# Four stacked graph layers on one core: in the attention layer, some second source blocks get a product of their own C in place of two products with B and A

## The chip, the cores and the metric

The program runs on one core of a Trainium2 chip. The time is device microseconds (us) of one execution; the kernel before took 4998.77 us (median of 10 executions, 4990.63 to 5002.31). The lower the better. One more execution was recorded with the profiler, and everything said of single instructions comes from it.

The engines of the core work side by side, each through its own list of instructions in order: PE multiplies matrices (a matmul streams its right operand against weights loaded before, and adds into PSUM), DVE does elementwise work on two inputs, ACT does activations and copies, POOL does some elementwise work and gathers, SP issues the transfers from HBM. [...]

## The reference

A graph of 6250 nodes with 206250 directed edges (100000 random pairs in both directions, and a loop at every node) goes through four layers; after each, x = layernorm(x + layer(x)). The layer that matters here is the last one, attention with four heads of 32 columns:

```python
h = (x @ W).reshape(N, H, C)
a_src = jnp.sum(h * att_src, axis=-1)
a_dst = jnp.sum(h * att_dst, axis=-1)
logits = a_src[src] + a_dst[dst]
logits = jnp.where(logits > 0, logits, NEG_SLOPE * logits)      # 0.2
e = jnp.exp(logits - seg_max[dst])
denom = jax.ops.segment_sum(e, dst, num_segments=N)
msgs = h[src] * (e / (denom[dst] + EPS))[:, :, None]
out = jax.ops.segment_sum(msgs, dst, num_segments=N)
```

The exponential of a leaky sum falls into a factor of the source times a factor of the target, with one pair of factors where the sum is positive and another where it is negative. So a head's sums over edges are two products with 0/1-like matrices: the adjacency counts of the edges whose sum is positive (called B here), and of those whose sum is not (C = A - B), where A is the matrix of edge counts between a block of sources and a stretch of targets.

## The kernel before, in words

The adjacency counts A are made early in the kernel, in blocks of 128 sources, and kept in HBM as bf16 (`adj`). The attention layer (`attend`, from L1134) goes through 4 heads x 6 units of targets = 24 **steps**. A unit is 1024 targets, two groups of 512; the sixth unit of each head has 106 targets more (`more`), with small tiles `Am` and `Bm` and a PSUM tile `sm` of their own. Within a step a loop goes over the 49 source blocks of 128 nodes in **pairs** (`for b in range(0, NB, 2)`); this text numbers them by b/2, pairs 0 to 24, the last with one block alone. So there are 600 pairs.

The work of a pair, in the order in which it is written (no planner moves anything here; each engine goes through its list as the loop writes it):

- SP loads A for the pair three places later (L1283, four buffers).
- ACT makes `r` (L1320), one activation of 128x1024 for each block of the pair: 0 or very large, by the sign of the sum.
- DVE makes B = min(A, r) for both blocks in one instruction (L1327), and C = A - B for the first block only (L1329). `r`, `B` and `C` have two buffers each; a third tile of a name waits until the readers of the first are done.
- PE multiplies (L1347), each term once for each of the two groups, so ten matmuls of 512 columns: B of the first block with its table 0; B of the second block with its table 0; for the second block's other sum, B times `minus` (the negated table 1) and A times table 1, which together stand for C times table 1; and C of the first block with its table 1. With `more`, each of the five terms has a small matmul into `sm` as well (L1349).

After each pair, three "lanes" (`sums`, `news`, `ends`) each make one small piece of other work, written behind the pair's own instructions. `sums` closes the step before: at pair 1 ACT copies half of the finished sums out of PSUM (L1229), at pair 2 DVE copies the other half (L1232), then PE folds them with 16 small matmuls for each group (L1239) and DVE scales them (L1243 to L1248); and behind that it makes the next step's `ad` (four PE transposes, L1216, and an ACT copy, L1213 or L1221, for each group). `news` makes the next head's tables, in units 1 to 5 of each head but the last: DVE L1191, L1193 and L1201, ACT L1196, POOL L1198. `ends` finishes the rows in the last head, so that head has more DVE work than the others. The matmuls of a step sum into four PSUM tiles `s`; the pool of them has six.

Before the first step, on the way into the layer, the factors are made: `t` (whose tile is named "neg", L1168 and L1169) goes through two exponentials on ACT (L1170, L1171), and `s` (a tile of its own, L1174) through L1175 and L1176 into a third (L1177).

Of the kernel before, what the change touches and what calls it, by code (L numbers as in the profile page):

```python
# [9 lines left out]
F32 = mybir.dt.float32  # L10
BF16 = mybir.dt.bfloat16
# [7 lines left out]
P = 128  # L19
# [4 lines left out]
F = 512  # L24
D = 128
HEADS = 4
# [42 lines left out]
def kernel(  # L69
# [9 lines left out]
    nc = tc.nc  # L79
# [9 lines left out]
    NB = -(-N // P)  # L89
# [543 lines left out]
    def general():  # L633
        with ExitStack() as st:
# [12 lines left out]
            def edges(name, rows_of):  # L647
                with tc.tile_pool(name=f"{name}s", bufs=1) as ep, \
# [12 lines left out]
                    for b in range(0, N, F):  # L661
# [3 lines left out]
                        for t in range(T):  # L665
                            ohb = ep.tile([P, F], F32, name="ohb", bufs=2)
                            nc.vector.tensor_scalar(ohb[:, :n], wide[:, :n], float(b), node[:, t : t + 1],
                                                    op0=ALU.add, op1=ALU.is_equal)
                            for slot, M, terms in sums:
                                for k, term in enumerate(terms):  # L670
                                    nc.tensor.matmul(pss[slot, k][:M, :n], term(t), ohb[:, :n],
                                                     start=t == 0, stop=t == T - 1)
                        for slot, M, terms in sums:
                            for k in range(len(terms)):
                                a = acc[:M, slot + k, b : b + n]
                                nc.vector.tensor_add(a, a, pss[slot, k][:M, :n])

# [78 lines left out]
    def fast():  # L756
# [377 lines left out]
        def attend(acc, al):  # L1134


            M = 3 * (CH + 1)
            NP = -(-NB // 2)
            hn = acc[:, 0, 0 : NB * D].rearrange("p (b h c) -> p b h c", h=HEADS, c=CH)
            flat = acc[:, 1:3, :].rearrange("p k n -> p (k n)").bitcast(BF16)  # L1140
            US = (2 * NB + NB // 2) * M
            tabs = []
# [7 lines left out]
            with tc.tile_pool(name="f3c", bufs=1) as one, tc.tile_pool(name="f3", bufs=2) as ep, \  # L1150
# [19 lines left out]
                nc.scalar.activation(us[:, :, :, 0], t, AF.Exp)  # L1170
                nc.scalar.activation(us[:, :, :, 1], t, AF.Exp, scale=SLOPE)  # L1171
                nc.vector.tensor_scalar(bias, al[:, 0], BIG, None, op0=ALU.mult)
                s = one.tile([P, NB, HEADS], F32, name="s")
                nc.vector.tensor_add(s, al[:, 1], mids)  # L1174
                nc.vector.tensor_scalar(vs[:, :, :, 0], s, 1.0 - SLOPE, 0.0, op0=ALU.mult, op1=ALU.min)  # L1175
                nc.vector.tensor_scalar(vs[:, :, :, 1], s, SLOPE - 1.0, 0.0, op0=ALU.mult, op1=ALU.min)  # L1176
# [27 lines left out]
                def width(of):  # L1204
                    return sum(rows * nb for n0, rows, nb in of)

                def targets(k, h, n0, of, more):

                    to = one.tile([P, 2 * F + P], F32, name=f"ad{k % 2}")
                    last = None  # L1210
                    for m0, rows, nb in of + more:
                        if last is not None:
                            nc.scalar.copy(*last)  # L1213
                        pt = pps.tile([P, F], F32, name="na")
                        for j in range(nb):
                            nc.tensor.transpose(pt[:, j * rows : (j + 1) * rows],  # L1216
                                                al[:rows, 1, m0 // P + j, h : h + 1].to_broadcast([rows, P]),
                                                ident[:rows, :rows])
                        last = (to[:, m0 - n0 : m0 - n0 + rows * nb], pt[:, : rows * nb])
                        yield  # L1220
                    nc.scalar.copy(*last)  # L1221
                    ready[k] = to
# [30 lines left out]
                class Lane:  # L1253
# [15 lines left out]
                    def rest(self):  # L1269
                        while self.left:  # L1270
                            self.step(self.due)
# [24 lines left out]
                for k, (h, n0, of, more) in enumerate(steps):  # L1296
                    ad, n, m = ready.pop(k), width(of), width(more)
                    tab, minus = tabs[h % 2]
                    s = [[sps.tile([P, F], F32, name="s") for g in of] for _ in range(2)]
                    sm = rps.tile([P, 2, P], F32, name="sm") if more else None  # L1300
                    ns = -(-n // (2 * P))
                    w = n // ns
                    begun = set()
                    if k + 1 < len(steps):
                        sums.add(targets(k + 1, *steps[k + 1]))
                    if n0 == 0:
                        news.rest()
                    if n0 == units[min(1, len(units) - 1)][0] and h + 1 < HEADS:
                        news.add(tables(h + 1, groups))
                    for b in range(0, NB, 2):  # L1310
                        kk = min(2, NB - b)
                        while k == 0 and made < 4 * min(len(groups) + 1, b // 8 * 2 + 4):
                            next(first[made % 2], None)
                            made += 1
                        load(i + 3)
                        At, Am = A.pop(i), more_of.pop(i, None)
                        i += 1
                        r = ep.tile([P, 2, 2 * F + P], BF16, name="r")
                        for l in range(kk):
                            nc.scalar.activation(r[:, l, : n + m], ad[:, : n + m], AF.Relu,  # L1320
                                                 bias=bias[:, b + l, h : h + 1], scale=BIG)

                        def wide(x):
                            return x[:, :kk, :n].rearrange("p l (s q) -> p s l q", q=w)

                        bt = ep.tile([P, 2, 2 * F], BF16, name="B")
                        nc.vector.tensor_tensor(wide(bt), At[:, :ns, :kk, :w], wide(r), ALU.min)  # L1327
                        ct = ep.tile([P, 2 * F], BF16, name="C")
                        nc.vector.tensor_sub(ct[:, :n].rearrange("p (s q) -> p s q", q=w), At[:, :ns, 0, :w],  # L1329
                                             bt[:, 0, :n].rearrange("p (s q) -> p s q", q=w))  # L1330
                        if more:
                            bm = ep.tile([P, 3, P], BF16, name="Bm")
                            nc.vector.tensor_tensor(bm[:, :kk, :m], Am[:, :kk, :m], r[:, :kk, n : n + m], ALU.min)
                            nc.vector.tensor_sub(bm[:, 2, :m], Am[:, 0, :m], bm[:, 0, :m])
                        terms = [(0, tab[:, b, 0], lambda c0, c1: bt[:, 0, c0:c1], lambda: bm[:, 0, :m])]
                        if kk == 2:
                            terms += [
                                (0, tab[:, b + 1, 0], lambda c0, c1: bt[:, 1, c0:c1], lambda: bm[:, 1, :m]),
                                (1, minus[:, b // 2], lambda c0, c1: bt[:, 1, c0:c1], lambda: bm[:, 1, :m]),
                                (1, tab[:, b + 1, 1], lambda c0, c1: At[:, c0 // w : c1 // w, 1, :w], lambda: Am[:, 1, :m])]  # L1340
                        terms.append((1, tab[:, b, 1], lambda c0, c1: ct[:, c0:c1], lambda: bm[:, 2, :m]))
                        for j, (to, row, rhs, rest) in enumerate(terms):
                            row = row.rearrange("p k c -> p (k c)")
                            stop = b + 2 >= NB and all(q[0] != to for q in terms[j + 1 :])
                            for g, (m0, rows, nb) in enumerate(of):
                                c0, c1 = m0 - n0, m0 - n0 + rows * nb
                                nc.tensor.matmul(s[to][g][:M, : c1 - c0], row, rhs(c0, c1), start=to not in begun, stop=stop)  # L1347
                            if more:
                                nc.tensor.matmul(sm[:M, to, :m], row, rest(), start=not begun, stop=stop,  # L1349
                                                 skip_group_check=True)  # L1350
                            begun.add(to)
                        now += 1
                        for lane in (sums, news, ends):
                            lane.step(now)
                    sums.rest()
                    sums.add(close(h, of + more, [[s[to][g][:M, : of[g][1] * of[g][2]] for to in range(2)] for g in range(len(of))]
                                   + [[sm[:M, to, :m] for to in range(2)] for g in more]))
                    sums.due = now + 2
# [58 lines left out]
```

## Time and profile before

| what | value |
|---|---|
| median of 10 executions | 4998.77 us |
| the profiled execution, its own time | 4998.32 us |
| its span, first to last instruction | 4996.5 us |
| first matmul of the attention steps | 3413.71 us into the span |
| steps 1 to 17 (the rest of heads 0 to 2) | 3501.47 to 4545.36, 1043.89 us |
| one of these steps with 1024 targets | 59.4 to 61.0 us, by the starts of the first matmuls |
| one of these steps with 1130 targets (`more`) | 67.3 to 67.6 us |
| head 3, steps 18 to 22 | 59.4, 62.6, 63.5, 64.5 and 62.5 us |

A line of the profile's groups names the source line (L1327), the engine, the operation, the tile that it writes and those that it reads, how many there are, their busy time and the mean of one. In the timeline the columns are the start and the duration in us, then engine, line, operation and tiles, with the idle time before it in brackets and what ended that idle time. In the table of waits the columns are who waited, for what, the total in us, how often, and the longest. In the chain of waits each row is a start, a duration and what ran there, with x the number of instructions.

### The profile page before, as it was taken

What the parts mean: (1) busy time and instruction counts of PE and PEld (TensorE: products, weight loads), DVE (VectorE), ACT (ScalarE), POOL (GpSimd) and SP (SyncE); (2) the same over time, 40 slices, a digit from 0 to 9 for tenths busy, and PEclk for the clock granted to TensorE, in tenths of its full rate; (3) what the DMA queues carried; (4) which work ended last, traced back from release to release, by engine and by line L of the source; (5) the groups of instructions that cost most, each with busy time, mean ns of one, the idle gap of its engine ahead of it and who ended that gap; (6) DMA issues with size and microseconds to landing.
All of it is one profiled execution on the core that took longest, in us unless ns stands there. A gap on an engine that the chain in (4) does not pass through costs nothing. (4 is left out here: it accounts for less than half of the span.)

```text
span 4996.5 us, 90752 instructions
## 1 busy us (share of the span) xinstructions
PE 4716.9 (94%) x33855; PEld 3924.5 (79%) x33855; DVE 3020.2 (60%) x5084; ACT 2602.9 (52%) x3617; POOL 2010.6 (40%) x1966
## 2 busy tenths in 40 slices
PE   4999998999999999999999999996999999999994
PEld 3899997999999999999999988994556556556553
DVE  6888875344444444444444432225888888888998
ACT  4444443333333333333333321005998999999884
POOL 3333432777777777777777740001110110110000
PEclk9999999999999999999999999997999999999997
DMA  6333333555555555555555545553777777777773
GB/s 105 128 131 134 142 134 122 149 154 155 154 153 155 155 154 153 155 156 154 152 156 154 154 153 180 184 190 107 217 218 227 215 217 227 212 220 223 210 213 108
DMA packets 599589, 834.35 MB, mean 167 GB/s; under 512 B 119837, under 2 KB 484313, under 8 KB 594917
## 3 DMA queue, kind: packets, MB, share of 16 engines
q1 hardware_dynamic: 513077, 603.59, 39.1%
q0 software_dynamic: 85072, 224.21, 15.2%
q8 instruction: 272, 4.46, 0.4%
q14 instruction: 176, 1.44, 0.1%
q10 hardware_dynamic: 992, 0.66, 0.0%
HBM read 738.23 MB, written 89.88 MB: 166 GB/s over the span
## 5 line engine op out<-in xcount | busy, mean ns | idle before, releaser
L127 POOL DMA_INDIRECT g<-t,src_i x1617 | 1590.3, 983 | 506.4 <-issue 397.8
L1320 ACT ACTIVATE r<-ad,bias 128x1024 bf16<-128x1024 f32 (+1 forms) x1176 | 1276.6, 1155 | 90.1 <-DVE B L1327 55.8
L1347 PEld LDWEIGHTS <-acc 128*99 128x99 bf16 x5856 | 697.4, 126 | 604.6 <-issue 156.5
L1095 DVE TENSOR_TENSOR g<-g,pre 128x512 f32<-128x512 f32 x882 | 553.5, 642 | 1018.6 <-PE pre L1093 651.7
L1347 PE MATMUL s<-B,acc 128*99 128x512 bf16 x3504 | 884.6, 382 | 88.7 <-DVE B L1327 83.2
L1107 PE MATMUL seg<-oh,g 128*128 128x64 f32 (+1 forms) x6468 | 967.0, 272 | 0.1
L1107 PEld LDWEIGHTS seg<-oh,g 128*128 128x128 f32 (+1 forms) x6468 | 890.6, 193 | 24.3 <-issue 1.2
L1096 ACT ACTIVATE g<-g 128x512 f32<-128x512 f32 x882 | 508.4, 592 | 588.6 <-DVE g L1095 569.6
L1093 PE MATMUL pre<-W1s,eaT 128*128 128x256 f32 (+1 forms) x3234 | 777.6, 382 | 20.2 <-DVE g L1095 20.0
L1327 DVE TENSOR_TENSOR B<-A,r 128x2048 bf16<-128x2048 bf16 x600 | 723.2, 1205 | 117.9 <-ACT r L1320 91.4
L1093 PEld LDWEIGHTS pre<-W1s,eaT 128*128 128x128 f32 (+1 forms) x3234 | 582.2, 191 | 86.3 <-issue 22.5
L1107 PE MATMUL seg<-oh,ea 128*128 128x64 f32 (+1 forms) x3234 | 628.0, 276 | 0.0
L1084 ACT COPY eaT<-tp 128x512 f32<-128x512 f32 (+1 forms) x441 | 242.0, 549 | 705.1 <-PE tp L1082 695.5
L907 ACT CAST A<-pa 128x784 bf16<-128x784 f32 x400 | 324.5, 811 | 350.7 <-PE pa L904 350.5
L1198 POOL TENSOR_TENSOR xs<-xs,acc 128x264 f32<-128x264 f32 (+1 forms) x104 | 105.1, 1018 | 990.8 <-ACT acc L1196 969.4
L1107 PEld LDWEIGHTS seg<-oh,ea 128*128 128x128 f32 (+1 forms) x3234 | 493.7, 193 | 0.0
L798 PE MATMUL sum<-A,xs 128*128 128x256 bf16 (+1 forms) x3675 | 470.7, 274 | 0.4 <-ACT A L907 0.4
L1329 DVE TENSOR_TENSOR C<-A,B 128x1024 bf16<-128x1024 bf16 x600 | 430.9, 718 | 63.6 <-PE s L1347 0.8
L798 PE MATMUL sum<-A,acc 128*128 128x256 bf16 (+1 forms) x3675 | 409.3, 271 | 3.3 <-DMA A<-adj 3.3
L798 PEld LDWEIGHTS <-acc 128*128 128x128 bf16 x3675 | 355.1, 98 | 44.8 <-issue 4.8
L798 PEld LDWEIGHTS <-xs 128*128 128x128 bf16 x3675 | 358.9, 102 | 36.7 <-issue 0.6
L904 PE MATMUL pa<-oh,oh 128*128 128x98 bf16 x3200 | 356.0, 269 | 26.9 <-ACT A L907 22.4
(229 smaller groups left out, 4416.9 us busy)
## 6 DMA issues: line engine op xcount, KB each, us to landing
A<-adj SPq DMA_DIRECT2D x2304, 128.0 KB
ea<-in_edge_attr_dram SPq DMA_DIRECT2D x292, 256.0 KB
A<-adj SPq DMA_DIRECT2D x100, 704.0 KB
ea<-in_edge_attr_dram SPq DMA_DIRECT2D x146, 192.0 KB
g<-t,src_i POOLq DMA_INDIRECT x1617
Am<-adj SPq DMA_DIRECT2D x96, 128.0 KB
A<-adj SPq DMA_DIRECT2D x25, 320.0 KB
t<-y SPq DMA_DIRECT2D x24, 256.0 KB
```

Of the source, the lines that this page charges most:

```text
L127: nc.gpsimd.indirect_dma_start(out=to, out_offset=None, in_=table, in_offset=bass.IndirectOffsetOnAxis(ap=index[:K, t : t + 1], axis=0))
L798: nc.tensor.matmul(ps[:, :n], parts[part][:, b, :], a(b)[:, :n], start=k == 0, stop=k == 3 * NB - 1)
L904: nc.tensor.matmul(ps[:, o, q * LO : (q + 1) * LO], ohs[g][0][:, 2 * j + o, :, q], ohs[g][1][:, 2 * j + o, :, q], start=True, stop=True)
L907: nc.scalar.copy(A[sb][:, :, q0 : q0 + 2 * QI].rearrange("p k (o q) -> p k o q", q=QI), ps[:, :, : QI * LO].rearrange("p o (q k) -> p k o ...
L1093: nc.tensor.matmul(pre[:K, t, :], eaT[i][:, b + t, :K], W1s[:, 1, :], start=True, stop=True)
L1095: nc.vector.tensor_add(gb, gb, pre[:K, :n, :])
L1096: nc.scalar.activation(gb, gb, AF.Relu)
L1107: nc.tensor.matmul(ps[:, m, :], rows, oh[c][:K, a + t, :], start=a + t == 0 and m == 0, stop=a + t == T - 1, skip_group_check=True)
L1320: nc.scalar.activation(r[:, l, : n + m], ad[:, : n + m], AF.Relu, bias=bias[:, b + l, h : h + 1], scale=BIG)
L1327: nc.vector.tensor_tensor(wide(bt), At[:, :ns, :kk, :w], wide(r), ALU.min)
L1329: nc.vector.tensor_sub(ct[:, :n].rearrange("p (s q) -> p s q", q=w), At[:, :ns, 0, :w], bt[:, 0, :n].rearrange("p (s q) -> p s q", q=w))
L1347: nc.tensor.matmul(s[to][g][:M, : c1 - c0], row, rhs(c0, c1), start=to not in begun, stop=stop)
```

## The change

In pairs 2, 7, 12, 17 and 22 (b = 4, 14, 24, 34, 44) of every step of heads 0, 1 and 2, DVE makes C for both blocks of the pair, with a second instruction of the same shape. The second block's other sum is then one term, C times table 1, in place of the two terms with `minus` and A; the pair has four terms in place of five, and the C of both blocks come last. The tile pool is unchanged: "C" has two buffers, and such a pair takes both. With `more`, the small subtraction L1334 covers two rows in place of one (in `Bm`, four rows in place of three), and the small matmul of one term goes too. All other pairs, and head 3, are as before. Apart from that, `s` of the way in takes the tile "neg" of `t` in place of one of its own.

```diff
-                s = one.tile([P, NB, HEADS], F32, name="s")
+                s = one.tile([P, NB, HEADS], F32, name="neg")
...
-                        ct = ep.tile([P, 2 * F], BF16, name="C")
-                        nc.vector.tensor_sub(ct[:, :n].rearrange("p (s q) -> p s q", q=w), At[:, :ns, 0, :w],
-                                             bt[:, 0, :n].rearrange("p (s q) -> p s q", q=w))
+                        cc = kk if b % 10 == 4 and h + 1 < HEADS else 1
+                        ct = []
+                        for l in range(cc):
+                            ct.append(ep.tile([P, 2 * F], BF16, name="C"))
+                            nc.vector.tensor_sub(ct[l][:, :n].rearrange("p (s q) -> p s q", q=w), At[:, :ns, l, :w],
+                                                 bt[:, l, :n].rearrange("p (s q) -> p s q", q=w))
                         if more:
-                            bm = ep.tile([P, 3, P], BF16, name="Bm")
+                            bm = ep.tile([P, 4, P], BF16, name="Bm")
                             nc.vector.tensor_tensor(bm[:, :kk, :m], Am[:, :kk, :m], r[:, :kk, n : n + m], ALU.min)
-                            nc.vector.tensor_sub(bm[:, 2, :m], Am[:, 0, :m], bm[:, 0, :m])
+                            nc.vector.tensor_sub(bm[:, 2 : 2 + cc, :m], Am[:, :cc, :m], bm[:, :cc, :m])
                         terms = [(0, tab[:, b, 0], lambda c0, c1: bt[:, 0, c0:c1], lambda: bm[:, 0, :m])]
                         if kk == 2:
+                            terms.append((0, tab[:, b + 1, 0], lambda c0, c1: bt[:, 1, c0:c1], lambda: bm[:, 1, :m]))
+                        if kk > cc:
                             terms += [
-                                (0, tab[:, b + 1, 0], lambda c0, c1: bt[:, 1, c0:c1], lambda: bm[:, 1, :m]),
                                 (1, minus[:, b // 2], lambda c0, c1: bt[:, 1, c0:c1], lambda: bm[:, 1, :m]),
                                 (1, tab[:, b + 1, 1], lambda c0, c1: At[:, c0 // w : c1 // w, 1, :w], lambda: Am[:, 1, :m])]
-                        terms.append((1, tab[:, b, 1], lambda c0, c1: ct[:, c0:c1], lambda: bm[:, 2, :m]))
+                        for l in range(cc):
+                            terms.append((1, tab[:, b + l, 1], lambda c0, c1, l=l: ct[l][:, c0:c1], lambda l=l: bm[:, 2 + l, :m]))
```

## The prediction

> **What bounds the kernel now.** I read the page first, for the engines' shares; then the busy time in steps 1 to 17 alone, since all of the change but one line lies in heads 0 to 2; then who waits for whom there; then the chain of waits and the timeline through one whole step (step 9, 3989.97 to 4049.69).
>
> ```profile
> PE 4716.9 (94%) x33855; PEld 3924.5 (79%) x33855; DVE 3020.2 (60%) x5084; ACT 2602.9 (52%) x3617; POOL 2010.6 (40%) x1966
> ```
> ```profile
> 3501.47:4545.36 1043.89, 1010.18 (x5207) 614.43 (x5205) 919.50 (x1294) 961.73 (x1023) 89.21 (x78) 1.00 0.73 220
> ```
>
> The page says PE, with DVE at 60%. The second line (length, then busy PE, weight loads, DVE, ACT and POOL, the granted clock, DMA) says otherwise for the stretch that is changed: PE 97%, ACT 92%, DVE 88%. Three engines are nearly full, so what counts is who is late at which place. The waits of the stretch:
>
> ```profile
> PE s L1347 <- DVE B L1327: 25.2, 40, 1.2
> ACT r L1320 <- DVE B L1327: 28.3, 46, 1.6
> ACT ad L1213 <- PE na L1216: 29.8, 17, 2.1
> DVE B L1327 <- ACT r L1320: 52.7, 66, 2.2
> ```
>
> Of the 33.7 us in which PE is idle there, 25.2 end with DVE's B. ACT's `ad` waits once in each of the 17 steps for PE's transposes. So the limit changes hands within a step, and the chain through step 9 shows where:
>
> ```profile
> 3995.47 1.27 DVE sT L1232 x2
> 3996.74 1.14 DVE B L1327
> 3997.88 0.04 issue
> 3997.93 4.48 PE s L1347 x20
> ...
> 4010.15 6.49 PE s L1347 x30
> 4016.64 0.45 PE na L1216 x4
> 4017.09 0.02 issue
> 4017.12 0.59 ACT ad L1213
> 4017.70 2.08 ACT r L1320 x2
> ```
>
> DVE carries it into pair 3, PE from pair 3 to the transposes behind pair 9, ACT from `ad` to pair 22, and then DVE again over the seam into the next step. In every step of 1 to 17 the rows are the same within some tenths, so one step is a fair model of all.
>
> **The prices.** One matmul: the row "4010.15 6.49 PE s L1347 x30" gives 0.216 us. A changed pair drops two of ten: 0.43 us of PE. A C takes 0.69 us, but the instruction behind it starts 0.61 after it did (4009.71 to 4010.32). While POOL's `xs` runs, a C takes 0.97; over the stretch's 400 the mean is 0.723 beside a median of 0.692. So one more C costs DVE's queue 0.61 + 0.03 = 0.64 (bounds 0.61 and 0.89). It waits for no result of the C in front. With `more`, L1334 over two rows is nearest to L1333's 0.265 in place of 0.217: +0.05. Over 18 steps x 5 pairs that is 39 us off PE and 58 us onto DVE. What it does to the end is worked out by pair.
>
> **Pair 2 (DVE binds).** The rows of DVE and PE:
>
> ```profile
> 3994.57 0.97 DVE L1329 TENSOR_TENSOR C<-A,B 128x1024 bf16<-128x1024 bf16 x1
> 3995.47 1.27 DVE L1232 COPY sT<-s 99x512 f32<-99x512 f32 x2
> 3996.66 1.21 DVE L1327 TENSOR_TENSOR B<-A,r 128x2048 bf16<-128x2048 bf16 x1
> 3997.93 0.59 PE L1347 MATMUL s<-B,acc 128*99 128x512 bf16 x2 [1.09 <-DVE B L1327]
> ```
>
> From C of pair 2 over the two copies to B of pair 3 DVE isn't idle (0.00 to 0.04 us in steps 1 to 17), and PE stands idle 0.46 to 1.16 us until that B is done, starting 0.05 after it. The second C goes in front of the copies, so all of it arrives at PE; the 0.43 that PE saves in pair 2 only adds to its idle time. 17 x 0.64 + 3 x 0.05 = +11.0 us. Step 0 has 2.86 us of DVE idle there: nothing. From pair 3 to 11 PE has no idle time, so nothing takes this back.
>
> **Pair 7 (PE binds).** Here 0.43 could be gained. But three C's now share two buffers: C of pair 8 must wait until PE has read the first C of pair 7.
>
> ```profile
> 4009.71 0.69 DVE L1329 TENSOR_TENSOR C<-A,B 128x1024 bf16<-128x1024 bf16 x1
> 4009.99 1.48 PE L1347 MATMUL s<-B,acc 128*99 128x512 bf16 x6
> 4011.60 1.23 DVE L1327 TENSOR_TENSOR B<-A,r 128x2048 bf16<-128x2048 bf16 x1
> ```
>
> The rows are C of pair 8, PE's pair 7, B of pair 9. PE frees that buffer after six of eight matmuls, at 4009.99 + 5 x 0.216 + 0.38 = 4011.45, so with 0.05 to notice it C of pair 8 starts at 4011.50, 1.79 later than now. Queued behind it are the scaling (L1243 to L1248) and B of pair 9, with 0.10 idle to absorb it: B ends 1.69 later, at 4014.52. PE took that B at 4014.32 and would now be free at 4013.89, so it starts at 4014.57: 0.25 late instead of 0.43 early. The same arithmetic gives +0.79, +0.30, +0.25, +0.34 in units 1 to 4, +0.16 in unit 5, +0.03 in unit 0, and -0.43 in step 0, where C of pair 8 comes 5.4 us after that read. Sum 3 x 1.68 + 3 x 0.16 + 2 x 0.03 - 0.43 = +5.1 us. Bounds: -7.7 (18 x 0.43, if the buffer comes free in time) and +9 (0.5 a step). The wait is also in front of `r` of pair 11, but `ad` behind pair 11 waits for PE anyway.
>
> **Pairs 12, 17 and 22 (ACT binds, DVE just follows).** PE's saving is worth nothing: `r` ends 0.03 us before B starts. DVE's idle time from here, without the 0.10 that every C waits for its B, is 1.06, 0.98, 0.92, 0.42 us (units 1 to 4) between pairs 12 and 17: the C of pair 12 is absorbed but for 0.22 in unit 4. Between pairs 17 and 22 it is 0.16, 0.53, 0.58, 0.58, so 0.48, 0.11, 0.06, 0.28 are left when pair 22 adds its 0.64, and the idle time before B of pair 23 (0.37, 0.06, 0, 0) takes little. At the seam there is none:
>
> ```profile
> 4044.81 1.22 DVE L1327 TENSOR_TENSOR B<-A,r 128x2048 bf16<-128x2048 bf16 x1
> 4046.07 4.26 ACT L1320 ACTIVATE r<-ad,bias 128x1024 bf16<-128x1024 f32 x4 [0.33 <-DVE B L1327]
> 4047.03 0.68 DVE L1327 TENSOR_TENSOR B<-A,r 128x1024 bf16<-128x1024 bf16 x1
> 4048.42 1.22 DVE L1327 TENSOR_TENSOR B<-A,r 128x2048 bf16<-128x2048 bf16 x1
> ```
>
> ACT's `r` of the next step's pair 0 waits for B of pair 23 to free its buffer (0.03 us behind it), and behind that `r` stand the one of pair 1, the copies `sT`, the `r` of pair 2 and so pair 2's B. The lag arrives whole at the idle PE of pair 3: 0.75, 0.69, 0.70, 0.92 in units 1 to 4, 3 x 3.06 = 9.2 us; 0.65 and 0.83 in steps 6 and 12; 0.82, 0.60, 0.82 in steps 5, 11, 17, where DVE also carries Bm; 0.15 in step 0, with 0.49 idle. Sum +13.1 us; bounds 0 and 54 x 0.64 = 35.
>
> **The way in.** `s` in the tile of `t` waits for the second exponential (3399.78 + 0.36) in place of starting at 3399.55, and behind it on DVE stand L1175, L1176 and the tables, on ACT the third exponential and `ad`: +0.7 us (bounds 0 and 0.8). SP and POOL get nothing new: A's buffers come free when DVE has read A, no later than now.
>
> **Sum.** 11.0 + 5.1 + 13.1 + 0.7 = +29.9 us on the profiled execution's 4998.3 (span 4996.5 and 1.8 around it, 0.5 below the median): 5028 us.
>
> [...]
>
> **Rivals.**
> - PE sets the pace and DVE's 12% of idle time holds the C's: 4998.3 - 39 = 4959 us. It needs 0.64 us of DVE slack at both places at which I find none; for it stands the 97%, against it the four rows of pair 2. Its milder form, gains in pair 7 and where PE has no wait in pairs 17 and 22 and nothing lost at the seam, ends near 4998.3 + 11 - 18 x 3 x 0.43 = 4986. Together 0.15.
> - The lags are absorbed at the seam and C's two buffers don't hold: pair 2's +11.0, the way in's 0.7 and pair 7's -7.7 give +4, 5002 us, no change to be told. It decides if B of pair 23 isn't what ACT waits for; in 15 of the 18 steps it is, and in the other three (`more`) it is Bm behind that B. 0.11.
> - DVE becomes the bound all through: all 90 C's at 0.64 = 58, 5057 us. Head 3, where DVE is 93% busy, takes 62.5 to 64.5 us a step and shows that such a state exists; against it stand 0.42 to 1.06 us of idle DVE after pair 12. 0.06.
> - That the change doesn't do what it says: the lists are written by the loops, so L1347 must lose 180 matmuls and C gain 90. Not counted.
>
> **How the numbers follow.** My forecast has 0.68, with a range of its own from 5010 (the seam takes half, pair 7 gives 0) to 5044 (C at 0.89). What a measurement can tell from no change is about 0.2%, 10 us. The forecast and the DVE bound are slower, 0.74; the absorbed case is the same, 0.11; the PE cases are faster, 0.15. Leaving out the faster cases and a part of the slowest, the range is 4995 to 5045.
>
> **What the changed profile would show.** PE's idle time before pair 3 up by about 1.8 us (0.43 saved, 0.64 and some 0.75 later); DVE idle with "PE s" as the releaser before C of pair 8, some 1.2 us each; PE waiting for B of pair 9, which it doesn't now; `r` of pair 0 still behind B of pair 23; a step with 1024 targets at 61.5 to 62.5 us instead of 59.4 to 61.0; head 3 unchanged. The prediction is wrong if B of pair 3 comes less than 0.5 us later against the step's last PE wait, or if steps get shorter.

## The result and the profile after

The changed kernel takes 5033.4 us (median of 8 executions, 5024.73 to 5042.28) against 4997.45 us for the kernel before (28 executions): 36 us more, a ratio of 1.0074 with a 95% interval of 1.0065 to 1.0082. It is slower, as forecast, by 36 us where 30 were forecast. The profiled execution took 5028.66 us, its span is 5026.9; of the difference, the attention steps (first to last matmul) make 1555.45 - 1518.95 = +36.5 us, and the layers before them, which the change doesn't touch, happened to be 6.8 us shorter in this execution (up to `bias`, 3392.61 against 3399.38).

Steps 1 to 17 run from 3497.84 to 4574.11 us here. First the busy time of that stretch (length, then PE, weight loads, DVE, ACT, POOL, the granted clock, DMA), then who waited for whom in it (total us, times, longest).

```profile
3497.84:4574.11 1076.27, 987.54 (x5020) 592.25 (x5020) 966.38 (x1379) 965.57 (x1024) 80.37 (x78) 1.00 0.71 213
```
```profile
PE s L1353 <- DVE B L1328: 69.6, 96, 1.9
ACT r L1321 <- DVE B L1328: 63.8, 75, 2.1
DVE B L1328 <- ACT r L1321: 26.8, 43, 1.2
ACT r L1321 <- DVE Bm L1337: 26.3, 24, 2.2
DVE C L1333 <- PE s L1353: 25.3, 33, 1.2
```

PE's busy time fell by 22.6 us (1010.18 to 987.54) and DVE's rose by 46.9 (919.50 to 966.38); the stretch is 32.4 us longer. (The 85 changed pairs of the stretch drop 85 x 0.43 = 37 us of matmuls; the busy time falls by less because the last matmul before an idle time counts for its whole 0.38 us, and there are more idle times now, 196 in place of 95.) PE's waits for DVE's B went from 25.2 to 69.6 us and ACT's from 28.3 to 63.8, while DVE waits half as long for ACT as before (52.7 to 26.8): DVE has become the one that is late. The 25.3 us in which C waits for PE are new. The places of step 9 again, pair 2 first (start, duration; DVE's rows, then PE's first matmul of pair 3):

```profile
4006.29 1.57 DVE L1333 TENSOR_TENSOR C<-A,B 128x1024 bf16<-128x1024 bf16 x2
4007.78 1.28 DVE L1233 COPY sT<-s 99x512 f32<-99x512 f32 x2
4008.98 1.21 DVE L1328 TENSOR_TENSOR B<-A,r 128x2048 bf16<-128x2048 bf16 x1
4010.24 0.38 PE L1353 MATMUL s<-B,acc 128*99 128x512 bf16 x1 [1.74 <-DVE B L1328]
```

Two C's stand in front of the copies, B of pair 3 comes 0.6 later after B of pair 2 (4.02 us in place of 3.42, start to start), and PE idles 1.74 us in place of 1.09. Pairs 7 to 9:

```profile
4023.82 0.69 DVE L1333 TENSOR_TENSOR C<-A,B 128x1024 bf16<-128x1024 bf16 x1 [1.19 <-PE s L1353]
4025.98 1.21 DVE L1328 TENSOR_TENSOR B<-A,r 128x2048 bf16<-128x2048 bf16 x1
4027.24 0.38 PE L1353 MATMUL s<-B,acc 128*99 128x512 bf16 x1 [0.87 <-DVE B L1328]
```

C of pair 8 waits 1.19 us for PE to read the first C of pair 7, and PE then idles 0.87 us for B of pair 9, where it didn't wait before. Pair 17 to 18 shows one thing that I hadn't counted, B of pair 18 at 1.69 us beside POOL's `xs`:

```profile
4045.61 1.29 DVE L1333 TENSOR_TENSOR C<-A,B 128x1024 bf16<-128x1024 bf16 x2
4046.67 0.76 POOL L1199 TENSOR_TENSOR xs<-xs,acc 128x264 f32<-128x264 f32 x1 [2.85 <-ACT acc L1197]
4046.82 1.69 DVE L1328 TENSOR_TENSOR B<-A,r 128x2048 bf16<-128x2048 bf16 x1
4048.57 1.46 PE L1353 MATMUL s<-B,acc 128*99 128x512 bf16 x6 [0.94 <-DVE B L1328]
```

And the seam, where `r` of the next pair 0 waits for B of pair 23, 0.71 us now, 0.33 before:

```profile
4058.54 1.22 DVE L1328 TENSOR_TENSOR B<-A,r 128x2048 bf16<-128x2048 bf16 x1
4059.79 4.26 ACT L1321 ACTIVATE r<-ad,bias 128x1024 bf16<-128x1024 f32 x4 [0.71 <-DVE B L1328]
```

### The profile page after: what moved, and what is told of

Read it like the earlier page. It is cut to its first block, busy times and chain, and to the rows that moved or that the text cites. A ratio compares the mean times of both kernels' runs of the same rounds, so it can differ in the third digit from the quotient of the medians.

```text
span 5026.9 us, 90243 instructions
## 1 busy us (share of the span) xinstructions
PE 4688.7 (93%) x33660; PEld 3896.8 (78%) x33660; DVE 3068.9 (61%) x5174; ACT 2605.3 (52%) x3617; POOL 2002.6 (40%) x1966
## 5 line engine op out<-in xcount | busy, mean ns | idle before, releaser
L1353 PEld LDWEIGHTS <-acc 128*99 128x99 bf16 x5676 | 676.4, 126 | 665.3 <-issue 239.6
L1353 PE MATMUL s<-B,acc 128*99 128x512 bf16 x3324 | 845.8, 382 | 139.2 <-DVE B L1328 132.7
L1333 DVE TENSOR_TENSOR C<-A,B 128x1024 bf16<-128x1024 bf16 x690 | 484.8, 710 | 94.4 <-PE s L1353 32.6
L1353 PE MATMUL s<-C,acc 128*99 128x512 bf16 x1380 | 402.2, 381 | 0.6 <-DVE C L1333 0.2
```

What stands on the lines that cost most here:

```text
L1333: nc.vector.tensor_sub(ct[l][:, :n].rearrange("p (s q) -> p s q", q=w), At[:, :ns, l, :w], bt[:, l, :n].rearrange("p (s q) -> p s q", q=w))
```

## How the runs are read

Every pair starts with a matmul of its own, so the start of each pair can be compared between two profiles, and a difference that grows between two pairs has reached PE there. The table adds up, over steps 1 to 17, what each stretch of pairs gained or lost against the kernel before; step 0 and head 3 stand by themselves. All in us, worked out from the starts of the matmuls in one profiled execution of each kernel.

| run | attention | step 0 | pairs 0-3 | 3-7 | 7-10 | 10-17 | 17-22 | 22 to end | head 3 |
|---|---|---|---|---|---|---|---|---|---|
| the change | +36.5 | +2.5 | +11.1 | -0.7 | +8.3 | +1.3 | +8.5 | +3.9 | +1.6 |
| PE's saving alone | -7.9 | -1.8 | +0.4 | +0.1 | -7.5 | -0.6 | -0.3 | +1.3 | +0.6 |
| DVE's C's alone | +26.1 | -0.6 | +11.0 | -0.5 | 0.0 | +1.2 | +8.8 | +4.2 | +2.1 |
| the change, own buffer | +23.0 | -0.7 | +11.3 | +4.3 | -6.4 | +0.7 | +8.8 | +2.9 | +2.1 |
| pair 2 alone | +11.0 | -0.1 | +10.8 | -0.5 | 0.0 | +0.4 | -0.1 | +0.3 | +0.2 |
| pair 7 alone | -2.1 | -0.3 | +0.7 | -0.1 | -5.7 | +1.0 | +2.0 | -1.0 | +1.3 |
| pair 17 alone | +5.9 | -0.5 | -0.5 | -0.1 | 0.0 | -0.2 | +9.4 | -4.2 | +1.9 |
| pair 22 alone | +8.1 | -1.0 | -0.7 | +0.1 | 0.0 | -0.2 | 0.0 | +8.4 | +1.4 |
| no C in pair 2 | -17.5 | -0.7 | -10.2 | -2.4 | 0.0 | +0.2 | +0.9 | -0.4 | -4.9 |
| no C in pair 2, pair 7 changed | -20.3 | -0.5 | -10.7 | -2.0 | -4.0 | +0.3 | 0.0 | +0.7 | -4.0 |

A column can differ by 1 to 2 us without any doing of the edit: head 3, which the first eight rows leave as it was, differs by +0.2 to +2.1. In the changed kernel (+1.6) one stretch at half clock lies there (granted 0.50 from 4919.95 to 4923.36 us), 1.22 us after PE had waited 1.50 us for B. PE's saving alone, DVE's C's alone, the change with its own buffer and pair 7 alone were run on another chip, on which the kernel before takes 5445.16 us: the granted TensorE clock is lower there ahead of the attention steps (0.94 for the whole execution against 0.98 on the first, with 1.00 in steps 1 to 17 on both). The attention steps run at the same speed on both (in head 3, 90 to 93% of the pairs agree within 0.01 us), so the table holds across them. The other runs were made on chips with 4995.55 and 4993.34 us for the kernel before. Ratios are always against the kernel before on the same chip; the change itself was not run on the slower chip, so its buffers are compared by the attention steps. The runs without a C in pair 2 keep `s` as the kernel before has it, but for the one that also changes pair 7; all others have it in the tile "neg", as the changed kernel does.

## PE's saving by itself, and DVE's price by itself

In all 90 pairs the product with `minus` is left out and no second C is made (the diff is against the changed kernel, as are the others unless it is said):

```diff
-                        cc = kk if b % 10 == 4 and h + 1 < HEADS else 1
+                        cc = kk if False else 1
...
-                                (1, minus[:, b // 2], lambda c0, c1: bt[:, 1, c0:c1], lambda: bm[:, 1, :m]),
+                                *([] if b % 10 == 4 and h + 1 < HEADS else [
+                                    (1, minus[:, b // 2], lambda c0, c1: bt[:, 1, c0:c1], lambda: bm[:, 1, :m])]),
```

> The 90 pairs of the change lose one of their five terms on PE (the product of minus and B, two matmuls of 512 columns, 0.43 us), and DVE makes no second C. The sum of the second block's other half is left out of the output in these pairs. This is PE's saving by itself. My theory: PE sets the pace only from pair 3 to the transposes behind pair 9, so only the saving in pair 7 arrives: 18 x -0.43 = -7.7, with the way in +0.6, about -7 us against the kernel before (4983 to 4993). The rival (PE at 97% sets the pace everywhere): 90 x -0.43 = -39, about 4959 us.

Ratio 0.9989 (0.9964 to 1.0015); attention -7.9 us. Its busy line for steps 1 to 17:

```profile
3948.31:4985.54 1037.23, 981.62 (x5020) 592.35 (x5020) 919.13 (x1294) 962.27 (x1024) 88.28 (x78) 1.00 0.75 221
```

PE is busy 28.6 us less in the stretch than before (1010.18) and the stretch is 6.7 us shorter (1043.89). Step by step the gain is 0.43 to 0.48 us at pair 7 in every one of the 17, and nothing that lasts at pairs 2, 12, 17 and 22. That is what the theory says, and PE's pace as the limit of all pairs (-39) is out.

Then the other half: the second C is made, into a place of its own, and nothing reads it; PE does its ten matmuls.

```diff
+                spare = [W1s.rearrange("p k h -> p (k h)").bitcast(BF16)]
+                taken = 0
...
-                            ct.append(ep.tile([P, 2 * F], BF16, name="C"))
+                            if l:
+                                ct.append(spare[taken % len(spare)])
+                                taken += 1
+                            else:
+                                ct.append(ep.tile([P, 2 * F], BF16, name="C"))
...
-                        if kk > cc:
+                        if kk == 2:
...
-                        for l in range(cc):
+                        for l in range(1):
```

> The second C of the 90 pairs is made, into a place of its own (the space of the W1 table, which only the fallback branch would read again), and nothing reads it; PE does its ten matmuls as before. This is DVE's price by itself, without the C buffers. My theory: pair 2 costs 17 x 0.6 and the lag over the seam some 13 us, pair 7 costs nothing since PE is late there by more than 1 us: +24 us, about 5021 us (5013 to 5029). The rival that the C buffers are the cause of the loss: 4998 us. The rival that DVE is the bound all through: 90 x 0.61 = +55, 5052 us.

Ratio 1.0041 (1.0017 to 1.0065), +22 us by the interval's middle; attention +26.1 us.

```profile
3933.50:5002.02 1068.52, 1013.77 (x5206) 614.35 (x5206) 967.62 (x1379) 965.62 (x1024) 82.16 (x78) 1.00 0.73 215
```

DVE's 48 us more work (967.62 against 919.50) make the stretch 24.6 us longer, with PE's work as before. The table says where: +11.0 into pair 3, nothing at pair 7, +13 between pair 17 and the seam. So most of the loss is DVE's queue at two places, and half of DVE's added time is hidden at the others.

## The two buffers of C

The change with the second C in a place of its own (the `spare`, `taken` and `ct.append` lines of the diff above, all else as in the change):

> The changed kernel with one edit: the second C of a pair goes to a place of its own (the space of the W1 table), so the C of the next pair needn't wait until PE has read the first one. My theory: the +8 us measured between pairs 7 and 10 and the +2.2 in step 0 turn into 18 x -0.43; pair 2 and the seam stay as they are (+10.6 and +12.4): about +16 us against before, 5013 us (5007 to 5019). The rival that the buffers don't matter: 5033 us, as the changed kernel.

Ratio 1.0041 (1.0020 to 1.0062); attention +23.0 us instead of +36.5. Between pairs 7 and 10 the +8.3 turned into -6.4, and step 0 went from +2.5 to -0.7. The 14.7 us between pairs 7 and 10 were the buffers' doing, and of step 0's 3.2 at least a part. About +16 was expected (8 to 20 by the range of times), so this missed, because something new came in at pair 3 of steps 1, 7 and 13: 1.4 us each, the table's +4.3. In step 7, with PE's rows first and then PE busy, the granted clock, DMA share and GB/s in windows there:

```profile
4317.36 0.59 PE L1359 MATMUL s<-W1s,acc 128*99 128x512 bf16 x2
4319.69 2.63 PE L1359 MATMUL s<-B,acc 128*99 128x512 bf16 x6 [1.74 <-DVE B L1330]
4323.53 1.46 PE L1359 MATMUL s<-B,acc 128*99 128x512 bf16 x6
```
```profile
4318.00:4320.00 2.00, 0.31 (x2) 0.95 0.89 257
4320.00:4321.00 1.00, 1.00 (x4) 0.50 0.60 193
4321.00:4322.00 1.00, 1.00 (x4) 0.50 0.05 15
4322.00:4323.00 1.00, 1.00 (x4) 0.50 0.00 0
4323.00:4324.00 1.00, 1.00 (x6) 0.89 0.09 16
```

After PE's 1.74 us of idle time the clock is granted by half for some 3.4 us (0.20, 3.00 and 0.22 by the windows), and six matmuls take 2.63 us instead of 1.46. The buffers are shown as the cause of the loss at pair 7; without these 4.3 us this run would stand at +18.7. (The tile W1s in the first row is the second C of pair 2.)

## One pair at a time

Only pair 7 (`b == 14`), its second C in a place of its own:

> As the run before, but only pair 7 is changed in each step of heads 0 to 2; pairs 2, 12, 17 and 22 are as in the kernel before. My theory: only the pair in which PE is the limit is left, 18 x -0.43 = -7.7 and the way in +0.6: -7 us, about 4990 us (4986 to 4994). The rival that a second C on DVE costs its 0.6 us wherever it stands: 18 x (0.6 - 0.43) = +3, 5001 us.

Ratio 0.9997 (0.9979 to 1.0015); attention -2.1 us. The 0.43 arrives at pair 7 in every step (0.48 with `more`), so the price of 0.6 wherever a C stands is out. But less than half is left at the end: in three steps with `more` 0.37 is lost again at pair 9; in single steps DVE waited for a late A (1.28 us before pair 19 of step 3), or B met POOL's `xs` (1.69 to 1.72 us at pairs 17 and 19 of steps 2 and 14); and head 3, which the edit leaves as it was, took 1.3 more. The gain is real where it is made and too small to survive; by time it can't be told from none.

Only pair 2, and only pair 17, and only pair 22 (`b == 4`, `b == 34`, `b == 44`), in the same way, each with one profiled execution:

> Only pair 2 is changed as in the diff, in heads 0 to 2, its second C in a place of its own. Measured by the attention steps in the profile, first to last matmul, against 1518.95 us before. My theory: DVE isn't idle between C of pair 2 and B of pair 3, so each of 17 steps loses 0.6 us there, as the changed kernel showed: +10 us (9 to 12). If PE were the limit: 18 x -0.43 = -8.

> Only pair 17 is changed in each step of heads 0 to 2, its second C in a place of its own. Measured by the attention steps in the profile, first to last matmul, against 1518.95 us in the kernel before. In the changed kernel PE's matmuls of pair 18 come about 0.6 us late in most steps and stay late to pair 22. My theory: DVE and ACT catch up before the seam (0.16 to 0.58 us of idle DVE time by pair 22 and a little behind it), so by pair 3 of the next step most of it is gone: 0 to +4 us. The rival that PE carries the delay on: 18 x 0.5 = +9 us.

> Only pair 22 is changed, its second C in a place of its own; same measure. My theory: there is no time left to catch up before the seam, where r of the next pair 0 waits for B of pair 23: 0.64 less the idle DVE time in front of that B (0.37, 0.06, 0, 0 in units 1 to 4), so 3 x 2.1 + 2 x 0.45 + 3 x 0.6 = +9 us (6 to 11). The rival that the seam has slack and pair 22 matters only together with pair 17: 0 to +3 us.

Pair 2 alone costs 11.0 us, 0.6 in nearly every step between pairs 2 and 3 (9.6 of the table's 10.8; 1.0 of the rest came before pair 2 of step 1 alone). Pair 22 alone costs 8.1, all of it behind pair 22. Pair 17 alone costs 9.4 us at PE up to pair 22, of which 4.2 are given back at the seam: 5.2. The sum of 5.9 also holds 1.3 for one late transfer at pair 2 of step 11 (DVE waits 1.98 us for A) and 1.9 in head 3, which it leaves as it was. So the delay at pair 17 doesn't vanish as I had it, nor does it all stay. The single pairs add up: 11.0 + 5.9 + 8.1 = 25.0 beside the 26.1 of DVE's C's alone, in which pair 7 costs nothing. Pair 12 wasn't run by itself; the column of pairs 10 to 17 leaves +1.3 at most for it.

## The opposite of the change where DVE is late

If DVE is late before pair 3 and PE idles there, the opposite should win. On the kernel before, with `s` and `Bm` as they were, pair 2 of all steps makes no C at all, and the first block too gets two products (the diff is against the kernel before):

```diff
+            minus4 = [flat[:, 2 * US + k * M : 2 * US + (k + 1) * M].rearrange("p (k c) -> p k c", c=CH + 1) for k in range(2)]
...
+                        if b0 == 4:
+                            nc.vector.tensor_scalar(minus4[h % 2], tab[:, 4, 1], -1.0, None, op0=ALU.mult)
...
+                        cc = kk if False else 1
+                        ct = []
+                        for l in range(0 if b == 4 else cc):
...
+                            if b != 4:
+                                nc.vector.tensor_sub(bm[:, 2 : 2 + cc, :m], Am[:, :cc, :m], bm[:, :cc, :m])
...
-                        terms.append((1, tab[:, b, 1], lambda c0, c1: ct[:, c0:c1], lambda: bm[:, 2, :m]))
+                        if b == 4:
+                            terms += [
+                                (1, minus4[h % 2], lambda c0, c1: bt[:, 0, c0:c1], lambda: bm[:, 0, :m]),
+                                (1, tab[:, b, 1], lambda c0, c1: At[:, c0 // w : c1 // w, 0, :w], lambda: Am[:, 0, :m])]
+                        for l in range(0 if b == 4 else cc):
+                            terms.append((1, tab[:, b + l, 1], lambda c0, c1, l=l: ct[l][:, c0:c1], lambda l=l: bm[:, 2 + l, :m]))
```

> The opposite of the change at the place where DVE is the limit, on the kernel before: in pair 2 of every step, all heads, DVE makes no C at all; the first block too gets two products, B with a negated table (one more small DVE instruction a head) and A with table 1, so PE has twelve matmuls there in place of ten. My theory: B of pair 3 comes 0.61 earlier and PE, which stands idle 0.46 to 1.16 us in front of it, has 0.43 more to do: a gain of the smaller of 0.61 and that idle time less 0.43, 3 x (0.5 + 0.5 + 0.61 + 0.38) + 2 x 0.55 = 7 us in heads 0 to 2 and about 2 in head 3, so attention at 1510 (1507 to 1514) and a ratio of about 0.998. The rival that PE at 97% is the limit: 23 x 0.43 = +10 us.

4973.33 us against 4995.55: ratio 0.9958 (0.9944 to 0.9971), 22 us faster than before and faster than both kernels. Attention -17.5 us, twice what was expected. Step 9, DVE and then PE:

```profile
3984.42 1.28 DVE L1236 COPY sT<-s 99x512 f32<-99x512 f32 x2
3985.92 1.23 DVE L1331 TENSOR_TENSOR B<-A,r 128x2048 bf16<-128x2048 bf16 x1 [0.22 <-DVE sT L1236]
3986.71 0.59 PE L1361 MATMUL s<-A,acc 128*99 128x512 bf16 x2
3987.20 1.02 PE L1361 MATMUL s<-B,acc 128*99 128x512 bf16 x4
```

PE goes from pair 2 (twelve matmuls) into pair 3 at 3987.20 without a gap. I had set the gain too low at one point: the idle time in brackets counts from the end of the last matmul, which is 0.38 after its start, while the next may start 0.216 after it; so PE had 0.16 us more room than the brackets said, and the steps with 1024 targets gained 0.54 to 0.89 at this place. The `more` steps gained 1.2 to 1.35 where I had nothing. In the kernel before, PE waits three times there, before pair 3 for B and in pairs 2 and 3 for `Bm` as well, and in this run none of the three is left (step 5 of the kernel before):

```profile
3748.29 0.21 PE L1349 MATMUL sm<-Bm,acc 128*99 128x106 bf16 x1 [0.30 <-DVE Bm L1333]
3750.87 0.59 PE L1347 MATMUL s<-B,acc 128*99 128x512 bf16 x2 [0.46 <-DVE B L1327]
3751.85 0.21 PE L1349 MATMUL sm<-Bm,acc 128*99 128x106 bf16 x1 [0.39 <-DVE Bm L1333]
```

Head 3 gained 4.9 instead of 2.

The same with pair 7 changed as in the change, its second C in a place of its own; and the same without that, but with no C in pairs 7, 12, 17 and 22 of head 3 either, where DVE has more work:

> The run before together with pair 7 changed as in the diff, its second C in a place of its own: C goes from DVE to PE where DVE is the limit and from PE to DVE where PE is. My theory: 9 us from pair 2 and up to 7.7 from pair 7 (5.7 of it arrived between pairs 7 and 10 in the run with pair 7 alone, and 2 at the end of attention): attention at 1506 us (1502 to 1512), ratio about 0.9975. The rival that PE is the limit: +10 - 7.7 = 1521 us.

> The run without C in pair 2 (ratio 0.9958, attention 1501.5 us), and in head 3 no C in pairs 7, 12, 17 and 22 either: in the head where DVE is 91 to 95% busy the opposite of the change in all its five pairs. My theory: 6 steps x 4 pairs, each worth up to 0.61 of DVE and at least the 0.2 by which it exceeds PE's 0.43, so -5 to -14 us beside that run: attention at 1492 (1487 to 1497), ratio about 0.994. The rival that head 3 is held up by its layernorm's chains and not by DVE's queue: no gain beside that run, or a loss of up to 24 x 0.43 = 10 us.

The first takes 4970.92 us, ratio 0.9956 (0.9943 to 0.9970); attention -20.3. The second takes 4976.49 us against 4993.34, ratio 0.9957 (0.9944 to 0.9971); attention -20.8, of which head 3 makes 8.2 instead of 4.9. Both miss what was expected of them. The first was expected at 1506 us of attention and took 1498.66, but 17.5 of its 20.3 are the run without C in pair 2, and pair 7 adds only 2.8 of up to 7.7: it keeps 4.0 up to pair 10, and head 3, which it doesn't touch, came out 0.9 worse. The second was to gain 5 to 14 us beside the run without C in pair 2 and gained 3.3: in head 3 the 0.43 that PE has to do more shows up in full at pair 7 of every step, and four of the six steps get it back by pair 10. Neither can be told from the run without C in pair 2 alone by its time.

## Why the prediction was right

The forecast of 5028 us met 5033.4, and the loss came at the places named. Not every term held: one is mis-sized, one has the wrong sign, and one came out right in its sum with parts that were not.

- **Pair 2, +11.0.** Measured +11.1 into pair 3, 0.6 in nearly every step, and +11.0 with this pair alone. The step held as written, and the opposite edit gained where this one lost.
- **Pair 7, +5.1, of it +5.6 in steps 1 to 17.** The mechanism, a C that waits for its buffer, is in the profile with 1.19 us and B of pair 9 late behind it; a buffer of its own takes it away. By units: +0.79, +0.30, +0.25, +0.34 were worked out for units 1 to 4, +0.80, +0.28, +0.60, +0.27 came. Two units were mis-sized. In unit 3 (+0.25 against +0.60) L1249, queued behind that C, takes 0.62 us beside POOL's `xs` in each of the three steps, where it took 0.29. In unit 5 (+0.16 against +0.87) PE waits in pair 9 for B and then 0.38 more for `Bm`, which stands behind it in DVE's queue; 0.54 of the 0.87 come there. Sum +8.3.
- **Step 0, -0.3 (-0.43 at pair 7, +0.15 at the seam).** This term was wrong: +2.5. I looked at the wait of pair 8's C only. The second C of pair 7 itself waits, for PE to read the C of pair 6, and in step 0 PE is far behind:

```profile
3433.05 0.69 DVE L1333 TENSOR_TENSOR C<-A,B 128x1024 bf16<-128x1024 bf16 x1 [0.94 <-PE s L1353]
```

  The second C's of pairs 2, 17 and 22 wait 1.90, 1.22 and 1.30 us in that step in the same way. Behind that of pair 7 on DVE stand the tables' products, on which the ACT casts of the first tables wait. With its own buffer step 0 lost nothing. How much of the 2.5 is each wait's isn't shown: step 0 also had the granted clock at half for 31.0 us, against 29.5 before (0.83 on the mean of the step in both). In steps 1 to 17 too the second C of pair 7 waits for the C of pair 6, 0.06 to 0.81 us, which the prediction left out.
- **Pairs 17 and 22 and the seam, +13.1, of it +12.9 in steps 1 to 17.** Measured +12.4 between pair 17 and the end of the step. The sum is right, by luck in part, for its split isn't: I let the delay of pair 17 run out before pair 22 but for 0.06 to 0.48 us, and at PE it stands at 0.5 us or so at once and comes back by less than half at the seam. Two rows were missing. PE has no idle time between pairs 18 and 22 (step 9), so what it loses there it keeps until somebody else is later. And `xs` on POOL met B in place of C: B at 1.69 to 1.73 us instead of 1.22 came 15 times in steps 1 to 17, 5 times before, ten times 0.48 us. I had priced a collision at 0.03 us, by C's mean, which fell meanwhile from 0.729 to 0.716 in the stretch.
- **PE's idle time before pair 3.** It was to rise by some 1.8 us, because the lag would arrive whole there. It rose from 0.87 to 1.63 on the mean of steps 1 to 17, and exactly as far with pair 2 alone; with pair 22 alone it stayed at 0.85. The lag of pairs 17 and 22 reaches PE before the seam, as the table's last columns of a step show, so this part of the path was wrong. And of the 0.43 that PE saves in pair 2, some 0.27 on the mean goes into waiting inside the pair, in step 9 for the second C.
- **The way in, +0.7.** From `bias` to the first `r` it takes 11.36 us instead of 10.74: +0.6.
- **PE's busy time, and B beside `xs`.** The busy time of the matmuls would have given -39 us; PE's saving alone brought 7.9, and the waits said the same. The 1.69 us of B in place of 1.22, beside an `xs` that started 0.15 before it and took 0.76, are 0.47 more for an overlap of 0.61. The term from it, ten such B's more at 0.48, is some 5 us of DVE's time, for which the forecast had its 0.03 a piece, 2.7 for 90 C's. What holds B up beside `xs` isn't shown.

That is 37 us in the attention steps and on the way in (35 from the bullets, 2 from the other columns); 36 by the medians. The rivals are out by their own runs: PE's pace by PE's saving alone, the absorbed lags by pair 22 alone (+8.1) and by the buffers' 1.19 us, DVE as the bound all through by DVE's C's alone (+26 of 55).

## What to carry to other kernels

With three engines at 88 to 97%, work moved from the fullest to another was paid here at the places where the other one is late, whatever the shares said. So go through one period of the loop, mark in each part who waits for whom, and put the edit only where the receiving engine has idle time and the giving one has none. A second tile from a pool of two was also a wait for the reader of the tile before it (1.19 us for C of pair 8), for this instruction and for the next user of the pool. And before adding to a queue, try the opposite at its worst place: here that was worth 22 us.

## What the runs showed of the hardware

In step 7 of the change with its own buffer an idle time of 1.74 us on PE was followed by some 3.4 us at a granted clock of 0.50 (the windows from 4318 to 4324 us above). In step 7 of the changed kernel the same idle time at the same pair wasn't (clock 1.00; PE, then the windows around it):

```profile
3886.02 1.46 PE L1353 MATMUL s<-B,acc 128*99 128x512 bf16 x6 [1.74 <-DVE B L1328]
```
```profile
3884.00:3886.00 2.00, 0.28 (x2) 0.03 (x1) 1.96 (x3) 1.48 (x4) 0.44 (x1) 1.00 0.83 262
3886.00:3888.00 2.00, 1.98 (x10) 1.16 (x10) 1.93 (x2) 2.00 (x2) 0.49 (x1) 1.00 0.42 133
```

In head 3 of the changed kernel an idle time of 1.50 us (up to 4918.73), with one of 0.39 behind it, was followed by a granted clock of 0.50 from 4919.95 to 4923.36, 3.41 us. So the length of one idle time doesn't decide it by itself, and what does isn't shown: no run shifted a start on purpose. In the run with its own buffer, pair 3 of steps 1, 7 and 13 lost 1.4 us each beside the idle time itself.

The attention steps of two chips agreed within 0.01 us in most pairs that weren't touched (90 to 93% of those in head 3), though the whole kernel took 9% longer on one of them.
